# A perceiver layer with routed experts: the first expert's first block of rows is put together on chip by matrix products, and the expert counts are taken earlier

## The chip, the cores and the metric

The kernel runs on one core of one Trainium2 chip. Its time is the device time of one execution in microseconds (us). The core has five engines that run side by side, each with its own queue of instructions in a fixed order: TensorE (PE, with PEld for its weight loads) multiplies matrices, VectorE (DVE) and ScalarE (ACT) work on elements, GpSimd (POOL) does some element work and issues transfers, SyncE (SP) issues transfers. In the profile a name with a q at its end (PEldq, ACTq) stands for the engine's sequencer: register loads, waits and branches.

## The reference, cut to what matters

There are 8 x 64 = 512 tokens of 512 features. Three stages are added one after the other onto the tokens x:

```
x = x + cross_attention(layernorm(x), context)   # 8 contexts of 1601 rows
x = x + self_attention(layernorm(x))             # within each group of 64 tokens, 8 heads
x = x + experts(layernorm(x))

# experts, for each token:
logits = xn @ router_w.T + router_b              # 8 experts
val, idx = top_k(logits, 2);  weight = softmax(val)
out = sum over the two experts e of weight * (silu(h1) * h2) @ w2[e].T + b2[e]
      where h1, h2 = split(xn @ w1[e].T + b1[e])  # 2 x 2048 hidden
```

The reference runs all experts on all tokens and picks two. The kernel runs each expert only on the tokens that chose it. All arithmetic is in float32.

## The kernel before, in words

**Tiles.** The 512 tokens are NTT = 4 tiles of P = 128 tokens, tile t in `xs[t]`. Features are ND = 4 blocks of 128.

**Attention and routing.** For each tile there are generators: `scores` and `average` (cross attention), `mix`, `attend` and `route`. `run` interleaves them: each yields an estimate of how long it should be left alone, and `run` keeps a clock of the estimated product time. All products and transposes of this stage go through `matmul` (line 205) and `transpose` (line 201), which chain each one behind the one before it, so TensorE's order is the order in which they are written down. The order on the other engines is the compiler's scheduler's. Tiles 0 and 1 follow each other inside `others`, beside the cross attention of later tiles; tile 2 and then tile 3 come at the end. Tile 3's buffers lie in a pool of their own (`beside`), opened when the cross attention is over.

**route(t).** A layernorm gives `xn` (named `xr`), four transposes and four small products give the logits. VectorE ranks the 8 experts of each token and writes a 0/1 mask of the two chosen (`masks`, L548). Then `pos` counts, by products with a triangle (`tri`) and with ones over earlier tiles, how many earlier tokens chose the same expert. `told[:, 0]` (L570) is that place plus `e * 512`, `told[:, 1]` the softmax weight. From these come `place` (L580) and `weight` (L581), and two indirect transfers (L583, on POOL) scatter the rows of `xn` into `sorted_x` in device memory, where the rows of expert e start at row `e * 512`. Last, `tg` turns the weights around, ScalarE copies them to `gT`, the product `mm` with `b2` is added to `xs[t]` (L603).

**Counts.** After all stages, four products with a column of ones (`cnt`, L704) sum the masks, and VectorE writes them as integers to `counts` (L705). Each of PE, ACT, DVE and POOL loads all eight into registers, one at a time (L888).

**Experts.** Each expert has 12 weight panels of 1 MB, 8 of w1 and 4 of w2, read by SP (`load_panel`, L153) into two pools: `early` holds 9 of each 17 panels, and its first filling is issued right after the cross attention, `late` holds 8. For expert e and block j of 128 of its rows, `level(e, j, xT)` branches on the count: with at most 64 rows in the block `narrow` is run, else `dense`, and after `dense` perhaps `level(e, j + 1)`. `load_rows_of` (L725, on POOL) reads 128 rows of `sorted_x`, behind all scatters; `turn` (L740, L751) transposes them. Rows of block 0 are read up to two experts ahead and turned one ahead; those of block j + 1 are read while block j is computed. For expert 0 the rows are read and turned inside the chosen arm (`xn0` or `xd0`). `dense` makes 16 products groups `h` (L769), each closed by a Silu on ScalarE (L777) and a product on VectorE (L780), with two `h` buffers, then 16 wide products `o` (L791), copied by ScalarE (L795) and written to `sorted_y`. `narrow` does the same for 64 rows (L812, L843).

**End.** Both result rows of each token are gathered from `sorted_y`, multiplied with their weights and added to `xs[t]`.

Of the kernel before, what the change touches and what calls it, by code (L numbers as in the profile page):

```python
# [9 lines left out]
F32 = mybir.dt.float32  # L10
AF = mybir.ActivationFunctionType
ALU = mybir.AluOpType
# [3 lines left out]
P = 128  # L16
# [4 lines left out]
def tile_perceiver_layer(  # L21
# [27 lines left out]
    nc = tc.nc  # L49
    B, T, D = x.shape  # L50
    S = context.shape[1]
    NT = B * T
    NTT = NT // P
    ND = D // P
    H = 8
    HD = D // H
    E = b2.shape[0]
# [9 lines left out]
    const = ctx.enter_context(tc.tile_pool(name="const", bufs=1))  # L67
    small = ctx.enter_context(tc.tile_pool(name="small", bufs=2))


    ident = const.tile([P, P], F32, name="ident")
# [4 lines left out]
    xs = [const.tile([P, D], F32, name=f"xs{t}") for t in range(NTT)]  # L76
# [21 lines left out]
    b2_sb = const.tile([E, D], F32, name="b2_sb")  # L98
# [15 lines left out]
    for e in range(1, E):  # L114
# [8 lines left out]
        channel_multiplier=-1,  # L123
    )
    ones = const.tile([P, P], F32, name="ones")
    nc.gpsimd.memset(ones, 1.0)

    first = const.tile([P, E], F32, name="first")
    for e in range(E):
        nc.gpsimd.memset(first[:, e : e + 1], float(e * NT))  # L130
    masks = const.tile([P, NTT, E], F32, name="masks")
    place = const.tile([P, NTT, 2], mybir.dt.int32, name="place")
    weight = const.tile([P, NTT, 2], F32, name="weight")
    counts = const.tile([1, E], mybir.dt.int32, name="counts")
    scatters = []

# [34 lines left out]
    with ExitStack() as attn:  # L173
        wide_const = attn.enter_context(tc.tile_pool(name="wide_const", bufs=1))
        wpool = attn.enter_context(tc.tile_pool(name="wpool", bufs=5))
        tok = attn.enter_context(tc.tile_pool(name="tok", bufs=2))
        wide = attn.enter_context(tc.tile_pool(name="wide", bufs=1))
        ps = attn.enter_context(tc.tile_pool(name="ps", bufs=1, space=PSUM))
# [25 lines left out]
        def matmul(out, lhsT, rhs, **flags):  # L204
            in_line(nc.tensor.matmul(out, lhsT, rhs, **flags))  # L205
            columns = math.prod(out.shape[1:])
            clock[0] += max(0.12, columns * (1.8e-3 if out.shape[0] > T else 1.0e-3))
# [8 lines left out]
        def bank(t, shape, use, name):  # L216
            if t < NTT - 1 or not cross_done:
                tag, bufs = {"turn": ("tr", 1), "few": ("s", 1)}.get(use, ("mm", 2))
            else:
                tag, bufs = {"turn": ("ctr", 2), "few": ("csc", 1), "left": ("ctr", 2)}.get(use, ("av", 1))  # L220
            return ps.tile(shape, F32, tag=tag, name=name, bufs=bufs)

        def buffers(t):
            return wide if t < NTT - 1 or not cross_done else beside[0]
# [155 lines left out]
        def average(t):  # L380

            nmax = small.tile([P, 1], F32, tag="nmax", name="nmax")
            nc.vector.tensor_reduce(nmax, mxs[t], AX.X, ALU.max, negate=True)
            ssum = small.tile([P, 1], F32, tag="ssum", name="ssum")
            nc.scalar.activation(scs[t], scs[t], AF.Exp, bias=nmax, accum_out=ssum)
            rsum = small.tile([P, 1], F32, tag="rsum", name="rsum")
            nc.vector.reciprocal(rsum, ssum)
            yield 5.0
            av = ps.tile([P, D], F32, tag="av", name="av")
            pTs = {}  # L390
            for j in range(NSB + 1):
                if j < NSB:
                    n = min(SB, S - j * SB)
                    w = min(P, n)
                    nch = -(-n // P)
                    tr = ps.tile([P, SB // P, P], F32, tag="ctr", name="ptr", bufs=2)
                    for c in range(nch):
                        s0 = j * SB + c * P
                        transpose(tr[:w, c, :], scs[t][:, s0 : s0 + w], ident)
                    pT = tpool.tile([P, SB // P, P], F32, tag="pT", name="pT")  # L400
                    nc.vector.tensor_copy(pT[:w, :nch, :], tr[:w, :nch, :])
                    pTs[j] = pT, w, nch
                    yield 1.0 if j == 0 else 0.0
                if j > 0:
                    pT, w, nch = pTs[j - 1]
                    for c in range(nch):
                        for i in range(2):
                            matmul(
                                av[i * T : (i + 1) * T, :],
                                pT[:w, c, i * T : (i + 1) * T],  # L410
                                cs[t, j - 1, i][:w, c, :],
                                start=(j == 1 and c == 0),
                                stop=(j == NSB and c == nch - 1),
                            )
                        yield 0.0
            avgs[t] = tok.tile([P, D], F32, tag="avg", name="avg")
            nc.vector.tensor_scalar(avgs[t], av, rsum, None, ALU.mult)

        avgs = {}
# [102 lines left out]

        masked = []


        def route(t):
            xn = buffers(t).tile([P, D], F32, tag="xr", name="xr", bufs=pair(t))
            layernorm(xn, xs[t])
# [21 lines left out]
            yield 2.0  # L550
            while len(masked) < t:
                yield 0.5
            pos = bank(t, [P, E], "few", "pos")
            for u in range(t + 1):
                matmul(
# [12 lines left out]
            nc.vector.reciprocal(norm, norm)  # L568
            nc.vector.tensor_scalar(told[:, 1, :], told[:, 1, :], norm, None, ALU.mult)
            nc.vector.tensor_tensor(told[:, 0, :], pos, first, ALU.add)  # L570
            both = small.tile([P, 2, 2, E], F32, tag="both", name="both", bufs=2)
            nc.vector.tensor_tensor(
                both,
# [8 lines left out]
            for c in range(2):  # L582
# [7 lines left out]
                for other in scatters:  # L590
                    tc.declare_no_dep(scatter.ins, other.ins, reason="no two tokens share a row")
                scatters.append(scatter)
            yield 2.0


            tg = bank(t, [E, P], "turn", "tg")
# [102 lines left out]
        weights = []  # L699
        run(others(), cross_steps, rest_of([2]), rest_of([3]))  # L700

        cnt = ps.tile([1, E], F32, tag="s", name="cnt")
        for t in range(NTT):
            matmul(cnt, ones[:, 0:1], masks[:, t, :], start=(t == 0), stop=(t == NTT - 1))  # L704
        nc.vector.tensor_copy(counts, cnt)  # L705

    with ExitStack() as ffn:
# [12 lines left out]
        def load_rows_of(e, j):  # L722
            r = rows.tile([P, D], F32, tag="r", name="r")
            at = e * NT + j * P
            read = nc.gpsimd.dma_start(out=r, in_=sorted_x[at : at + P, :])  # L725
            for scatter in scatters:
                tc.add_manual_dep(
                    read.ins,
                    scatter.ins.name,
                    mybir.DependencyInfo(  # L730
                        mybir.DependencyClass.Sync, mybir.DependencyReason.DATA
                    ),
                    reason="rows of any tile",
                )
            return r

        def turn(r, tag, after=None):
            tr = banks.tile([P, ND, P], F32, tag="t" + tag[0] + tag[-1], name="t")
            for k in range(ND):
                turning = nc.tensor.transpose(tr[:, k, :], r[:, k * P : (k + 1) * P], ident)  # L740
                if after is not None:
                    tc.add_manual_dep(
                        turning.ins,
                        after.ins.name,
                        mybir.DependencyInfo(
                            mybir.DependencyClass.NoSync, mybir.DependencyReason.DATA
                        ),
                        reason="TensorE's program",
                    )
            xT = cols.tile([P, ND, P], F32, tag=tag, name=tag, bufs={"xT": NB - 1, "x0": 2}.get(tag, 1))  # L750
            nc.vector.tensor_copy(xT, tr)  # L751
            return xT

# [112 lines left out]
        def level(e, j, xT):  # L866
            n = held[e]
            with arm(n <= j * P + P // 2, f"narrow_{e}_{j}"):  # L868
                foretell(n > j * P + P // 2, f"dense_{e}_{j}")
                narrow(e, j, xT or turn(firsts[0], "xn0"))  # L870
            if j == 0:
                tc.no_sync_barrier()
            with arm(n > j * P + P // 2, f"dense_{e}_{j}"):  # L873
                if j + 1 < NB:
                    foretell(n > (j + 1) * P, f"more_{e}_{j}")
                ahead = dense(e, j, xT or turn(firsts[0], "xd0"))
                if j + 1 < NB:
                    with arm(n > (j + 1) * P, f"more_{e}_{j}"):
                        level(e, j + 1, ahead)
            if j == 0:  # L880
                tc.no_sync_barrier()

        def ask(n):
            while len(panels) < min(E * NPAN, n):
                load_panel(len(panels))

        held = [
            nc.values_load(counts[0:1, e : e + 1], engines=engines, min_val=0, max_val=NT)  # L888
            for e in range(E)
        ]  # L890
        ask(EARLY + LATE)
        firsts = [load_rows_of(e, 0) for e in range(3)]

        tc.no_sync_barrier()
        level(0, 0, None)
        turned_rows = [None]
        for e in range(1, E):
            ask(e * NPAN + EARLY + LATE)
            if e + 2 < E:
# [86 lines left out]
```

## Time and profile before

| | |
|---|---|
| median of 3 runs (lowest to highest) | 905.05 us (903.5 to 906.7) |
| the profiled execution, its time | 905.28 us |
| its span, first to last instruction | 903.5 us |
| mean granted TensorE clock | 0.932 |
| TensorE matmul busy | 771.2 us (85%) |
| VectorE / ScalarE / GpSimd busy | 225.9 / 159.6 / 66.9 us |
| bytes moved | 165.99 MB, mean 184 GB/s |

A timeline row gives the start, the busy time, the engine, the line and operation, the output and inputs by the program's names, the shapes, the count, and in brackets the idle time of the engine before it and what ended it. A row of one line's instructions gives the shortest, median and longest duration in ns, then the first and last start in us. Every time in a row is counted from the span's start. The profile is one execution, so sums are made against its own 905.28 us.

In that execution expert 0 runs `dense` for one block, experts 1 and 2 `narrow`, 3 and 4 `dense`, 5 `narrow`, 6 three `dense` blocks and a `narrow` one, 7 a `dense` and a `narrow` one.

### The profile page before, as it was taken

To read this page: it belongs to the slowest core of one execution; us is meant where nothing else is said; L and a number is where in the kernel's file an instruction comes from. 1 tells how busy PE (TensorE), PEld (TensorE's weight loads), DVE (VectorE), ACT (ScalarE), POOL (GpSimd) and SP (SyncE) were. 2 spreads that over 40 slices of the span, in tenths; PEclk is the share of its full clock that TensorE was granted. 3 is DMA by queue.
4 is the path that set the end of the run, shared out by engine and by line. 5 is a ranking of instruction groups with operands and counts; after the bars stand their busy time and mean duration, and the time that the engine had idled before them with its cause. 6 is when DMAs were issued, how large, how long until landed. Compare 5 with 4: busy or idle time off the path is not lost. (4 is left out here: it accounts for less than half of the span.)

```text
span 903.5 us, 11522 instructions
## 1 busy us (share of the span) xinstructions
PE 771.2 (85%) x4794; PEld 517.8 (57%) x4794; DVE 225.9 (25%) x514; ACT 159.6 (18%) x324; POOL 66.9 (7%) x114
## 2 busy tenths in 40 slices
PE   3997997997999874399998896998899999969980
PEld 3883544444454442297454875945878786559450
DVE  2322265255342464111111110201111111101012
ACT  1123144034132123021110111100111110012000
POOL 5100200300000000100000000000000000000003
PEclk9998998999899997589999898999899999979995
DMA  9930970790420821900899957749940000062004
GB/s 304 363 135 1 366 298 0 266 415 7 151 71 1 332 88 57 396 15 2 324 403 417 403 206 302 294 155 419 408 181 24 3 24 1 1 266 93 12 5 142
DMA packets 40315, 165.99 MB, mean 184 GB/s; under 512 B 3552, under 2 KB 3568, under 8 KB 27936
## 3 DMA queue, kind: packets, MB, share of 16 engines
q1 hardware_dynamic: 31968, 136.34, 38.9%
q0 software_dynamic: 8256, 28.42, 8.3%
q8 instruction: 59, 0.97, 0.4%
q14 instruction: 32, 0.26, 0.1%
HBM read 142.34 MB, written 22.41 MB: 182 GB/s over the span
## 5 line engine op out<-in xcount | busy, mean ns | idle before, releaser
L769 PE MATMUL h<-x,panel 128*128 128x128 f32 x1024 | 124.6, 288 | 22.1 <-PEq L868 21.4
L769 PEld LDWEIGHTS h<-x,panel 128*128 128x128 f32 x1024 | 123.4, 204 | 23.9 <-issue 22.6
L780 DVE SCALAR_TENSOR_TENSOR g<-h,b_sb,g 128x128 f32<-128x128 f32 x112 | 39.3, 351 | 232.3 <-ACT g L777 232.3
L791 PE MATMUL o<-panel,g 128*128 128x512 f32 x224 | 97.3, 592 | 0.0
L791 PEld LDWEIGHTS o<-panel,g 128*128 128x128 f32 x224 | 42.1, 190 | 50.2 <-issue 50.2
L777 ACT ACTIVATE g<-h,b_sb 128x128 f32<-128x128 f32 x112 | 41.1, 367 | 150.3 <-PE h L769 150.2
L201 PEld LDWEIGHTS ctr<-ident,c 128*128 128x128 f32 x384 | 43.1, 145 | 40.6 <-DVE cT L333 13.3
L201 PE MATMUL ctr<-ident,c 128*128 128x128 f32 x384 | 54.4, 286 | 13.1 <-DMA c<-in_context_dram 11.5
L769 PEld LDWEIGHTS h<-xT,panel 128*128 128x128 f32 x512 | 57.3, 192 | 2.8 <-issue 2.8
L769 PE MATMUL h<-xT,panel 128*128 128x128 f32 x512 | 57.6, 276 | 1.2 <-ACTq L868 0.6
L205 PE MATMUL sc_ps<-cT,qk 128*64 128x512 f32 (+1 forms) x256 | 54.4, 524 | 4.9 <-ACT sc L326 4.9
L333 DVE COPY cT<-ctr 128x512 f32<-128x512 f32 (+1 forms) x52 | 34.8, 670 | 61.6 <-PE ctr L201 61.2
L812 PE MATMUL hn<-panel,x 128*64 128x512 f32 x192 | 49.3, 605 | 0.0
L331 ACT COPY cT<-ctr 128x512 f32<-128x512 f32 (+1 forms) x52 | 29.6, 570 | 111.2 <-PE ctr L201 111.2
L205 PE MATMUL av<-c,pT 128*64 128x512 f32 x192 | 48.4, 642 | 0.0
L843 PE MATMUL on<-panel,gT 128*64 128x256 f32 x320 | 38.6, 381 | 0.0
L833 DVE TENSOR_TENSOR gn<-hn,gn 128x256 f32<-128x256 f32 x20 | 8.5, 425 | 103.3 <-ACT gn L832 97.7
L205 PEld LDWEIGHTS mm<-hT,w 128*128 128x128 f32 x256 | 29.2, 192 | 8.8 <-DVE hT L237 8.8
L205 PE MATMUL mm<-hT,w 128*128 128x128 f32 x256 | 30.7, 278 | 4.0 <-DVE hT L237 4.0
L812 PE MATMUL hn<-panel,xT 128*64 128x512 f32 x128 | 32.2, 596 | 0.0
L769 PE MATMUL h<-xd,panel 128*128 128x128 f32 x256 | 31.3, 288 | 0.8 <-DVE xd L751 0.8
L843 PEld LDWEIGHTS on<-panel,gT 128*64 128x64 f32 x320 | 24.5, 137 | 12.9 <-issue 0.8
(175 smaller groups left out, 703.2 us busy)
## 6 DMA issues: line engine op xcount, KB each, us to landing
panel<-in_w_dram SPq DMA_DIRECT2D x96, 1024.0 KB, 15.6
c<-in_context_dram SPq DMA_DIRECT2D x24, 1024.0 KB, 10.9
sorted_x<-zeros POOLq DMA_DIRECT2D x8, 1024.0 KB, 19.1
sorted_y<-zeros POOLq DMA_DIRECT2D x8, 1024.0 KB, 18.9
r<-sorted_x POOLq DMA_DIRECT2D x15, 256.0 KB, 6.6
sorted_y<-y POOLq DMA_DIRECT2D x7, 256.0 KB, 6.8
cl<-in_context_dram SPq DMA_DIRECT2D x8, 130.0 KB
xs<-in_x_dram SPq DMA_DIRECT2D x4, 256.0 KB, 8.4
```

The costliest lines, as they stand in the source:

```text
L201: in_line(nc.tensor.transpose(out, in_, identity))
L205: in_line(nc.tensor.matmul(out, lhsT, rhs, **flags))
L331: nc.scalar.copy(dst, tr)
L333: nc.vector.tensor_copy(dst, tr)
L769: last = nc.tensor.matmul(h[:, half, :], w[:, k, half, (n % PC) * P : (n % PC + 1) * P], xT[:, k, :], start=(k == 0), stop=(k == ND - 1),)
L777: nc.scalar.activation(g[:, n, :], h[:, 0, :], AF.Silu, bias=b1_sb[:, col : col + 1])
L780: nc.vector.scalar_tensor_tensor(g[:, n, :], h[:, 1, :], b1_sb[:, col + NC1 : col + NC1 + 1], g[:, n, :], ALU.add, ALU.mult,)
L791: nc.tensor.matmul(o, g[:, n, :], w2_chunk(e, n), start=(n == 0), stop=(n == NC1 - 1))
L812: nc.tensor.matmul(h[q * s : (q + 1) * s].rearrange("p h c d -> p (h c d)"), xT[:, k, :s], w[:, k, :], start=(k == 0), stop=(k == ND - 1),)
L833: nc.vector.tensor_tensor(gn, h[:, 1], gn, ALU.mult)
L843: nc.tensor.matmul(o[q * s : (q + 1) * s, :], gT[:, m, c, i * s : (i + 1) * s], w2_chunk(e, n)[:, q * W : (q + 1) * W], start=(n == 0), st ...
```

## The change

Four things are done differently.

- In `route`, each tile builds `taken`, a 128 x 128 matrix of zeros and ones: row p has its one in the column of the place that token p has among expert 0's rows, if it chose expert 0 and the place is below 128. Four products of the blocks of `xn` with `taken` give those rows already transposed. They are summed over the tiles in `xT0`, which takes the place of the rows read back and turned for expert 0's block 0. The scatters stay.
- For the last tile, the counts are taken as soon as the masks are there, ahead of `pos`.
- Before expert 0, each engine loads the count of expert 0 alone. The other seven are loaded in one instruction behind expert 0, without the run-time check of their bounds.
- The last tile's `tg`, `gT` and `mm`, with the addition to its `xs`, move from `route` to behind expert 0. There `mm` uses the bank of the transposes of expert 1's and 2's rows (`tx0`).

In the built program TensorE has the last tile's work in the order cnt, pos, put, the load of one count, the branch. VectorE has the addition into `xT0` ahead of `place` and `weight` in tile 3, and between `told` and the softmax of tile 3 in tile 2. Behind expert 0 ScalarE has a table load and then the copy to `gT`; TensorE has tg, mm, eight transposes and the load of seven counts.

```diff
+    slots = const.tile([P, P], F32, name="slots")
+    nc.gpsimd.iota(
+        slots, pattern=[[1, P]], base=0, channel_multiplier=0, allow_small_or_imprecise_dtypes=True
+    )
+    xT0 = const.tile([P, ND, P], F32, name="xT0")
...
-            avgs[t] = tok.tile([P, D], F32, tag="avg", name="avg")
+            avgs[t] = tok.tile([P, D], F32, tag="avg", name="avg", bufs=1)
...
+            if t == NTT - 1:
+                while len(masked) < NTT:
+                    yield 0.5
+                cnt = bank(t, [1, E], "turn", "cnt")
+                for u in range(NTT):
+                    matmul(cnt, ones[:, 0:1], masks[:, u, :], start=(u == 0), stop=(u == NTT - 1))
+                nc.vector.tensor_copy(counts, cnt)
             pos = bank(t, [P, E], "few", "pos")
...
             nc.vector.tensor_tensor(told[:, 0, :], pos, first, ALU.add)
+            taken = buffers(t).tile([P, H, HD], F32, tag="lk", name="taken", bufs=2)
+            taken = taken.rearrange("p h d -> p (h d)")[:, :P]
+            nc.vector.tensor_scalar(
+                taken, slots, told[:, 0, 0:1], masks[:, t, 0:1], ALU.is_equal, ALU.mult
+            )
...
-            yield 2.0
+            yield 1.0
+            put = bank(t, [P, ND, P], "", "put")
+            for k in range(ND):
+                matmul(put[:, k, :], xn[:, k * P : (k + 1) * P], taken, start=True, stop=True)
+            if t == 0:
+                nc.vector.tensor_copy(xT0, put)
+            else:
+                nc.vector.tensor_tensor(xT0, put, xT0, ALU.add)
+            if t == NTT - 1:
+                gates.append(told)
+                return
+            yield 1.0
...
-        cnt = ps.tile([1, E], F32, tag="s", name="cnt")
-        for t in range(NTT):
-            matmul(cnt, ones[:, 0:1], masks[:, t, :], start=(t == 0), stop=(t == NTT - 1))
-        nc.vector.tensor_copy(counts, cnt)
...
-                narrow(e, j, xT or turn(firsts[0], "xn0"))
+                narrow(e, j, xT)
...
-                ahead = dense(e, j, xT or turn(firsts[0], "xd0"))
+                ahead = dense(e, j, xT)
...
-        held = [
-            nc.values_load(counts[0:1, e : e + 1], engines=engines, min_val=0, max_val=NT)
-            for e in range(E)
-        ]
+        def load_counts(first, end):
+            _, values = nc.values_load_multi_w_load_instructions(
+                counts[0:1, first:end],
+                engines=engines,
+                min_val=0,
+                max_val=NT,
+                skip_runtime_bounds_check_because="an expert has at most all tokens",
+            )
+            return list(values)
+
+        held = load_counts(0, 1)
         ask(EARLY + LATE)
-        firsts = [load_rows_of(e, 0) for e in range(3)]
-
+        firsts = [None] + [load_rows_of(e, 0) for e in (1, 2)]
         tc.no_sync_barrier()
-        level(0, 0, None)
-        turned_rows = [None]
+        level(0, 0, xT0)
+        held += load_counts(1, E)
+
+        tg = banks.tile([E, P], F32, tag="o", name="tg")
+        nc.tensor.transpose(tg, gates[0][:, 1, :], ident)
+        gT = small.tile([E, P], F32, tag="gT", name="gT", bufs=2)
+        nc.scalar.copy(gT, tg)
+        mm = banks.tile([P, D], F32, tag="tx0", name="mm")
+        nc.tensor.matmul(mm, gT, b2_sb, start=True, stop=True)
+        nc.vector.tensor_tensor(xs[NTT - 1], mm, xs[NTT - 1], ALU.add)
+        turned_rows = [xT0]
```

More of the change, by code (lines that the diff above doesn't have):

```diff
@@ L135, in tile_perceiver_layer @@
     scatters = []
+    gates = []
     dram = ctx.enter_context(tc.tile_pool(name="dram", bufs=1, space=bass.MemoryType.DRAM))
@@ L749, in turn @@
                     )
-            xT = cols.tile([P, ND, P], F32, tag=tag, name=tag, bufs={"xT": NB - 1, "x0": 2}.get(tag, 1))
+            xT = cols.tile([P, ND, P], F32, tag=tag, name=tag, bufs=NB - 1 if tag == "xT" else 2)
             nc.vector.tensor_copy(xT, tr)
```

## The prediction

> **What bounds the kernel now.** I read the page first: TensorE is busy in 85% of the span, so only work on its path counts. The chain of waits covers just the end (gather, add, store, 2% of the span), which the change leaves alone. So I read the timeline from the last tile's routing to the first expert's products.
>
> ```profile
> 365.99 0.17 DVE L548 TENSOR_SCALAR masks<-rank 128x8 f32<-128x8 f32 x1
> 366.21 0.59 PE L205 MATMUL pos<-masks,tri 128*128 128x8 f32 x2
> 369.94 0.97 POOL L583 DMA_INDIRECT sorted_x<-xr,place  x1 [0.30 <-issue]
> 371.24 0.14 DVE L705 CAST counts<-cnt 1x8 int32<-1x8 f32 x1
> 378.95 1.69 POOL L725 DMA_DIRECT2D r<-sorted_x  x3 [8.03 <-DMA sorted_x<-xr,place]
> 384.84 1.09 PE L740 MATMUL t<-ident,r 128*128 128x128 f32 x4 [13.96 <-DMA r<-sorted_x]
> 386.76 13.44 PE L769 MATMUL h<-xd,panel 128*128 128x128 f32 x96 [0.84 <-DVE xd L751]
> 390.69 1.28 ACT L777 ACT_TABLE_LOAD   x1 [22.22 <-PE h L769]
> 392.39 0.35 DVE L780 SCALAR_TENSOR_TENSOR g<-h,b_sb,g 128x128 f32<-128x128 f32 x1 [5.68 <-ACT g L777]
> ```
>
> See: the last scatter lands 8.03 us after its issue ends (378.94), then the rows are read back, and TensorE idles 13.96 us. The first product starts at 386.76, the first gate product at 392.39. The instructions of L868 (the test whether expert 0 is narrow) show a second wait beside it:
>
> ```profile
> L868 PEldq COMPARE_BRANCH  x1: 6102/6102/6102, 377.6 to 377.6; - x1
> L868 PEldq EVENT_SEMAPHORE  x1: 51/51/51, 383.8 to 383.8; - x1
> ```
>
> The branch goes to the dense arm and takes 6.1 us, to 383.7. It is hidden behind the read-back, but only just. From 435 us on the experts follow each other with TensorE 9.7 to 10 of 10 us busy, idle at taken branches alone: no expert waits for its panels. What the first expert gains passes to the end, and what is put between experts is lost in full.
>
> **1. The first expert's start: gain 9 us.** At the last tile, cnt now stands before pos and holds the three ones products, which before ran ahead of the mask (1.45 us at 364.84, six passes), behind it. From the mask at 366.16: these 1.45 and tri's 0.59 end at about 368.3, told at 368.5 (0.17). taken is a 128x128 TENSOR_SCALAR; the rows are 0.23 us for 128x8 (L569) and 0.55 for 128x512 (L158), so 0.3: 368.8. put is four products, eight passes; transposes x8 at half clock took 1.97 us (L201 pr_ps), so 1.9: 370.7. Adding to xT0 takes 0.69 (L603): rows ready at 371.45. tg, its copy, mm and xs no longer stand here.
>
> TensorE's queue behind put: one load of a count instead of eight (they took 371.4 to 377.6; one takes 0.30 to 0.55), then the branch. Sequencing runs ahead of the array, so the branch starts near 369.6. Five other long branches of this test and the next (L868, L873) took 3.2, 3.5, 5.7, 5.8 and 6.9 us. The Trainium skill (Runtime: NRT & Kernel Launch, "Instruction fetch mechanics") says that a taken branch to code outside the fetched blocks stalls for a DMA fetch. The trace agrees that it costs, with a 16 KB packet in the instruction queue at 381 to 382. By the rule the stall comes back in full, uncovered: 369.6 + 6.1 + 0.75 to the first product (as after other branches) = 376.4; by the shortest row, 3.2, or a block already there, 372.5. Either way the start is 10 to 14 us earlier.
>
> But that is not what decides. ScalarE's first Silu table load waits, besides the first product, for both scatters of the last tile (its buffer lies where their source lay). VectorE now does the xT0 add ahead of place and weight, which therefore end at 371.75 instead of 368.47, and the scatters are issued 3.3 us later, to about 374.2. Landing took 8.03 us behind the full panel queue (the DMA share is 1.0 until 382); the median over the four scatters of tiles 2 and 3 was 5.1. I take 8, the row nearest to it: 382.2 at most, say 381.5. Then table load 1.28 and Silu 0.37: first gate product at 383.2 instead of 392.39. With two h buffers TensorE has two blocks done 5.7 us after its start and waits for that. Gain **9.2**; between 12 (landing in 5) and 7 (see the clock, below).
>
> The read of row block 0 goes from POOL; two reads, one count and its branch remain there, and the reads start 3.3 us later. They are for experts 1 and 2, 60 us on: hidden. The other block's rows are needed 30 us later: hidden. SP's order is the same.
>
> **2. put at the earlier tiles: loss 4.9 us.** Each of tiles 0 to 2 adds taken, four products and a copy or add.
>
> ```profile
> 158.58 0.16 DVE L570 TENSOR_TENSOR told<-pos,first 128x8 f32<-128x8 f32 x1
> 158.81 0.24 PEld L205 LDWEIGHTS av<-c,pT 128*64 128x64 f32 x2 [0.62 <-issue]
> ...
> 341.10 0.17 DVE L570 TENSOR_TENSOR told<-pos,first 128x8 f32<-128x8 f32 x1 [0.54 <-PE pos L205]
> ...
> 342.31 0.20 DVE L490 RECIPROCAL sumh<-sumh 128x8 f32<-128x8 f32 x1
> ...
> 344.61 0.37 PE L201 MATMUL tg<-ident,told 128*8 128x128 f32 x1 [3.55 <-DVE told L569]
> ```
>
> Tiles 0 and 1 route while TensorE is full with the next tile's average (PE 10.0 of 10 us in 160:170, 9.3 to 10 in most later stretches). put stands behind two av products, ready for it at about 158.8, and taken ends at 159.2: a stall of 0.3 to 0.4 and eight passes of 0.11 to 0.2. 1.4 and 1.5 us; no slack follows, so all of it passes on. At tile 2 VectorE's order is told, taken, sumh, told, xT0 add, reciprocal. The add must wait for put, and tile 3's softmax is queued behind it: taken to 341.6, put (half clock, 1.9) to 343.5, add to 344.25, so the reciprocal starts then instead of at 342.31: 2.0 us on the serial chain of tile 3. Sum 4.9; 3.5 if a third is absorbed, 6 with a cold clock.
>
> **3. What is put between expert 0 and 1: loss 5 us.**
>
> ```profile
> 432.28 0.58 ACT L795 COPY y<-o 128x512 f32<-128x512 f32 x1 [13.80 <-PE o L791]
> 433.32 0.63 PE L740 MATMUL t<-ident,r 128*128 128x128 f32 x4 [1.07 <-PEq L878]
> 434.04 0.69 DVE L751 COPY x<-t 128x512 f32<-128x512 f32 x1 [14.58 <-PE t L740]
> 435.37 1.57 PE L812 MATMUL hn<-panel,x 128*64 128x512 f32 x4
> ```
>
> Before, two transposes and copies and then expert 1 at 435.37. Now tg comes first (0.3); ScalarE, which ended y at 432.86, loads a table (1.28) and copies gT (0.25) to 434.65; mm (1.12 at full clock) to 435.8; VectorE adds it to xs (0.69) to 436.55, and as mm and t share a bank the first transpose waits for that. Then transpose, copy and second transpose as before (about 1.85 with a colder clock) to 438.4. Behind its wait stands the load of seven counts, ahead of expert 1's branch. A single load took 0.30 at least, so seven would be 2.1 and the sum 5.7; the same section of the skill gives about 200 ns a register even in bulk, by which an estimate is 1.4 and the sum 5.0. I take 1.4, as it is one instruction; bounds 0.4 and 2.2. Expert 1 starts at 440.4: **5.0** later (4 to 6). Removing the eight loads at the front is counted in part 1.
>
> **Clock.** By windows of 2 us the granted clock is 0.50 from 362 to 390. The skill (TensorE: Matmul & The Clock Gate, "HAM oscillation") says that an idle gap over some 3.4 us halves the clock. This speaks against the change: if the products start at 372.5, TensorE has two blocks done by 378.2, idles until 383.5 for ScalarE and starts cold a second time; the row to price it is the cold start at 386.76, 4.6 us at half clock, 2.3 us lost. If they start at 376.4 the idle time is 1.5 us and nothing is lost. I count none and keep 2.3 for a rival. iota, slots, the smaller average buffer and the one-tile routing order elsewhere cost nothing: iota runs under the first loads, and each average is transposed before the next is written (274.48 against 296.9).
>
> **Sum.** 9.2 - 4.9 - 5.0 = 0.7 us slower than the profiled run's own 905.28 (span 903.5): 906.0. The median of the runs shown is 905.05, 0.23 lower, which is 905.8. I say **906**. About 0.3%, 2.7 us, is what a measurement here can tell from no change.
>
> **Rivals.** (a) Likeliest, 42%: as above, 906, own range 903.5 to 907.7: no measurable change. (b) Slower, 29%: the second cold start. Place: between the second and third h block of expert 0. Price 2.3 us, so 908.3; it decides once TensorE is idle there for more than about 3.4 us, that is when the branch costs under 5 us. For it: two of six long branches cost 3.2 and 3.5; against it: the one at this very place cost 6.1. (c) Faster, 18%: the puts are absorbed. If tiles 0 to 2 cost nothing, 906 - 4.9 = 901.1; with a scatter landing in 5 us, 3 more, 898. For it: TensorE has idle slots of 0.5 to 2.3 us before tile 1's and 3's transposes; against it: each of them is released by VectorE or ScalarE work that itself follows a product. (d) Slower, 9%: the code before the experts grew, so later branches meet other block borders. Two branches that cost 3.2 and 3.5 becoming 6.5 gives 6.3 us, 912; it can also go the other way. That the rows don't come from put at all, or that the panels bound the first expert, is excluded: its w1 panels lie in the pool filled from 296.9 us on.
>
> **How the numbers follow.** Faster 0.18 (c), slower 0.40 (b, d and 2% of both signs), same 0.42. Range: 901 (c without the early landing) to 911 (b with 6 and 6 for parts 2 and 3), leaving out the ends of (c) and (d).
>
> **What would show it.** Right: h<-xT0 starts 10 to 14 us earlier relative to the mask, the branch of L868's successor is uncovered, ScalarE's first table load ends an idle time released by the scatter, not by h; tile 3's reciprocal stands 2 us later; tg, mm and seven counts take 5 us before expert 1. Wrong: the table load follows the first product at once, so that the gain is 12 or more; or the average stage's end doesn't move.

## The result, and the profile after the change

The changed kernel takes 911.13 us (median of six runs), the kernel before 905.82. One of the six took 1208.93 us, with a granted clock of 0.64 instead of 0.92 to 0.93; the five others took 909.6 to 912.9 us (median 910.89), and with these five the changed kernel takes 1.0062 times as long, 95% interval 1.0036 to 1.0089. A second set of 16 runs gave a median of 910.79 against 904.12, ratio 1.0065 (1.0042 to 1.0087). So it is slower by 5 to 7 us; 906.0 was forecast, 0.7 us slower. The ratios, here and below, are not exactly the quotients of the medians beside them.

The timeline of the changed kernel around the last tile's mask and the first expert (start, length, engine, line, operation; in brackets the idle time before it and what ended it). `put`, `taken` and `xT` are the change's own; a "first gate product" is the first g of VectorE (L808), and a transfer "lands" when its data have arrived:

```profile
373.76 0.17 DVE L555 TENSOR_SCALAR masks<-rank 128x8 f32<-128x8 f32 x1
374.11 1.45 PE L213 MATMUL pos<-masks,ones 128*128 128x8 f32 x6
374.22 0.15 DVE L566 CAST counts<-cnt 1x8 int32<-1x8 f32 x1
376.63 2.07 PE L213 MATMUL put<-taken,xr 128*128 128x128 f32 x8 [0.64 <-DVE taken L589]
378.74 0.69 DVE L621 TENSOR_TENSOR xT<-put,xT 128x512 f32<-128x512 f32 x1 [0.98 <-PE put L213]
379.34 0.16 DVE L601 CAST place<-found 128x2 int32<-128x2 f32 x1
379.53 6.76 PE L797 MATMUL h<-xT,panel 128*128 128x128 f32 x32 [0.83 <-DVE place L601]
381.06 0.97 POOL L604 DMA_INDIRECT sorted_x<-xr,place  x1 [0.30 <-issue]
390.82 1.28 ACT L805 ACT_TABLE_LOAD   x1 [17.47 <-DMA sorted_x<-xr,place]
391.64 1.16 POOL L753 DMA_DIRECT2D r<-sorted_x  x2 [9.61 <-DMA sorted_x<-xr,place]
392.52 0.61 DVE L808 SCALAR_TENSOR_TENSOR g<-h,b_sb,g 128x128 f32<-128x128 f32 x2 [12.95 <-ACT g L805]
392.93 3.26 PE L797 MATMUL h<-xT,panel 128*128 128x128 f32 x14 [6.63 <-DVE g L808]
```

The mask stands 7.77 us later than before. The first h product follows it by 5.77 us instead of 20.77. Then ScalarE's table load waits until the scatters have landed, 8.79 us after the second one's issue ended (382.03), and TensorE, with two h blocks done, idles for 6.63 us. The first gate product comes 18.76 us after the mask instead of 26.40. Behind that idle time TensorE starts cold, that is at half clock, a second time (a window: length; busy time and count of PE, PEld, DVE, ACT and POOL; granted clock; share of the DMA engines; GB/s):

```profile
393.53:395.53 2.00, 2.00 (x11) 2.00 (x11) 0.00 (x0) 0.00 (x0) 0.54 (x1) 0.50 0.54 211
```

The instructions of the test for expert 0 (L896) on TensorE's queue; nanoseconds, then the start:

```profile
L896 PEldq COMPARE_BRANCH  x1: 459/459/459, 377.2 to 377.2; - x1
L896 PEldq EVENT_SEMAPHORE  x1: 51/51/51, 378.7 to 378.7; - x1
```

The branch that took 6.1 us before takes 0.46. It starts while put still runs, as the prediction had it, and is done before xT0 is. At tile 2 the same timeline shows VectorE waiting for put in front of tile 3's softmax, 3.39 us from told to the reciprocal instead of 1.21:

```profile
346.52 0.17 DVE L584 TENSOR_TENSOR told<-pos,first 128x8 f32<-128x8 f32 x1 [0.54 <-PE pos L213]
346.73 0.35 DVE L589 TENSOR_SCALAR taken<-slots,told,masks 128x128 f32<-128x128 f32 x1
347.22 2.05 PE L213 MATMUL put<-taken,xr 128*128 128x128 f32 x8 [0.73 <-DVE taken L589]
349.30 0.69 DVE L621 TENSOR_TENSOR xT<-put,xT 128x512 f32<-128x512 f32 x1 [1.53 <-PE put L213]
349.91 0.19 DVE L498 RECIPROCAL sumh<-sumh 128x8 f32<-128x8 f32 x1
```

Between expert 0 and expert 1 the timeline reads as follows; below it stands the row of the two count loads on TensorE's queue, one count and then seven (shortest/median/longest in ns, first and last start):

```profile
433.85 0.59 ACT L823 COPY y<-o 128x512 f32<-128x512 f32 x1 [13.80 <-PE o L819]
434.53 0.27 PE L933 MATMUL tg<-ident,told 128*8 128x128 f32 x1 [0.72 <-ACTq L906]
434.69 1.28 ACT L935 ACT_TABLE_LOAD   x1 [0.26 <-ACTq L906]
436.29 1.48 PE L937 MATMUL mm<-b_sb,gT 8*128 8x512 f32 x2 [1.49 <-ACT gT L935]
437.81 0.69 DVE L938 TENSOR_TENSOR xs<-mm,xs 128x512 f32<-128x512 f32 x1 [16.79 <-PE mm L937]
438.56 1.11 PE L768 MATMUL t<-ident,r 128*128 128x128 f32 x4 [0.79 <-DVE xs L938]
440.45 1.12 PE L768 MATMUL t<-ident,r 128*128 128x128 f32 x4 [0.78 <-DVE x L779]
442.84 1.97 PE L840 MATMUL hn<-panel,x 128*64 128x512 f32 x4 [1.27 <-issue]
```

```profile
L916 PEldq TENSOR_LOAD <-counts x2: 495/1121/1747, 376.6 to 440.5; - x2
```

Expert 1 starts 8.99 us after y instead of 3.09. The transposes run at half clock (1.11 and 1.12 us instead of 0.63 and 0.66), and the seven counts take 1.75 us on TensorE's queue, from 440.5 on, beside the second transpose.

The spans by stretches, the second profile of the changed kernel being one of the experiments:

| stretch (us) | before | after | again |
|---|---|---|---|
| start to the last mask | 365.99 | 373.76 | 372.60 |
| mask to first gate product | 26.40 | 18.76 | 17.91 |
| first gate product to first o product | 25.96 | 27.39 | 27.79 |
| first o product to expert 1 | 17.02 | 22.93 | 22.47 |
| expert 1 to the end | 468.13 | 466.36 | 467.33 |
| span | 903.5 | 909.2 | 908.1 |

For the first pair: 7.77 - 7.64 + 1.43 + 5.91 - 1.77 = 5.70.

### The profile page after: what moved, and what is told of

The parts are those of the page before. It is cut to its first block, busy times and chain, and to the rows that moved or that the text cites. A ratio compares the mean times of both kernels' runs of the same rounds, so it can differ in the third digit from the quotient of the medians.

```text
span 909.2 us, 11533 instructions
## 1 busy us (share of the span) xinstructions
PE 781.3 (86%) x4822; PEld 526.1 (58%) x4822; DVE 229.0 (25%) x521; ACT 161.0 (18%) x325; POOL 66.6 (7%) x114
## 5 line engine op out<-in xcount | busy, mean ns | idle before, releaser
L808 DVE SCALAR_TENSOR_TENSOR g<-h,b_sb,g 128x128 f32<-128x128 f32 x112 | 39.2, 351 | 243.6 <-ACT g L805 243.5
L797 PE MATMUL h<-xT,panel 128*128 128x128 f32 x768 | 91.1, 283 | 8.7 <-DVE g L808 6.6
L797 PEld LDWEIGHTS h<-xT,panel 128*128 128x128 f32 x768 | 90.4, 200 | 10.8 <-DVE g L808 6.8
L213 PE MATMUL mm<-w,hT 128*128 128x512 f32 x64 | 28.5, 599 | 2.8 <-DVE hT L245 2.8
```

What stands on the lines that cost most here:

```text
L797: last = nc.tensor.matmul(h[:, half, :], w[:, k, half, (n % PC) * P : (n % PC + 1) * P], xT[:, k, :], start=(k == 0), stop=(k == ND - 1),)
L808: nc.vector.scalar_tensor_tensor(g[:, n, :], h[:, 1, :], b1_sb[:, col + NC1 : col + NC1 + 1], g[:, n, :], ALU.add, ALU.mult,)
```

## The experiments

All ratios are against the kernel before, run on the same chip in the same set, with 95% intervals. The changed kernel's own ratio, to compare them with, is 1.0065.

**Rows apart.** My theory: the wait for the scatters holds the first expert. The rival: something else would hold it next.

```diff
-            xn = buffers(t).tile([P, D], F32, tag="xr", ...)
+            rows_of = buffers(t) if buffers(t) is wide else last_rows[0]   # a pool that is never given up
+            xn = rows_of.tile([P, D], F32, tag="xr", ...)
```

> The changed kernel, with the last tile's normalized rows in a place of their own, so that what the experts' pools reuse is no longer read by the two scatters. Nothing is left out. Theory (the scatters' landing holds ScalarE's first table load, and through it the first gate product): the table load follows the first h block, the first gate product comes about 5.7 us after the first h product as it did before the change, about 19.4 us after the mask's start minus 8: near 385.3 instead of 392.5, and with no idle time over 1 us TensorE does not fall back to half clock a second time. 7.2 and 1.4 us: 902.5 us, faster than before the change by about 3. Rival (another thing holds the table load, or what is won is lost again in a later wait for the second row block or the panels): within 2 us of the changed kernel's 911.

901.03 us, ratio 0.9970 (0.9949 to 0.9991). Its timeline:

```profile
375.37 5.43 PE L799 MATMUL h<-xT,panel 128*128 128x128 f32 x32 [0.83 <-DVE place L602]
379.16 1.28 ACT L807 ACT_TABLE_LOAD   x1 [9.96 <-PE h L799]
381.26 25.28 PE L799 MATMUL h<-xT,panel 128*128 128x128 f32 x224 [0.46 <-DVE g L810]
```

The table load is released by the first h block. The first gate product (380.86) comes 11.26 us after the mask (369.60), TensorE idles 0.46 us, and the h products from there to the next transposes take 25.12 us instead of 26.54 to 26.95. The theory holds: 8.5 to 8.9 us of the changed kernel's stretch from mask to o (45.7 and 46.2 us, here 37.2) were this wait and the cold start behind it. What makes the wait is the pool. In both built programs g lies at the same bytes of each partition (134432 to 142624) and so does xr (153568 to 155616); they do not overlap, and all that differs is the pool that xr belongs to. In the changed kernel it is `beside`, in whose place g lies and which is given up as a whole. The prediction, with "its buffer lies where their source lay", put this too narrowly.

**Bias last, and counts at once.** These two price what stands between expert 0 and 1.

```diff
             level(e, 0, turned_rows[e])
+        tg ... gT ... mm ... xs[NTT - 1] += mm        # moved from before the loop over experts 1 to 7
```

> The changed kernel, with the last tile's bias product (tg, its copy gT, mm and the add to xs) not between expert 0 and 1 but behind the last expert, where TensorE has nothing to do while the last rows come back. Nothing is left out. Theory (this product stands on the path in full): expert 1's first product comes 3.5 to 4.5 us earlier after the end of expert 0; 907 us. The load of seven counts stays where it was and keeps its 1.7 us. Rival (the seven counts are what the gap consists of, and the product lies beside them): under 1 us, 910 to 911.

906.41 us, ratio 1.0015 (0.9996 to 1.0035). From the first o product to expert 1 it is 18.62 us: 3.9 to 4.3 less, within the 3.5 to 4.5 expected.

```diff
-        held = load_counts(0, 1)
+        held = load_counts(0, E)
...
-        held += load_counts(1, E)
```

> The changed kernel, with all eight counts loaded by one instruction ahead of expert 0 instead of one there and seven behind expert 0. Nothing is left out. Theory (the seven cost 1.75 us on TensorE's queue between the experts; eight at once cost about 1.95 ahead of expert 0, where TensorE's sequencer waits for put and the xT0 add): 1.3 to 1.8 us faster, 909.4. Rival (eight delay the branch and so the first product by 1.4 us, no gain): 911.

905.96 us, ratio 1.0017 (0.9998 to 1.0036): some 4 us less, where 1.3 to 1.8 were expected. Between the experts it is 21.45 us, 1.0 to 1.5 less, a little under what was expected. The rest came from an order that I had not meant to change: VectorE now does place and weight ahead of the xT0 add.

```profile
374.32 0.16 DVE L602 COPY weight<-found 128x2 f32<-128x2 f32 x1
374.69 0.97 POOL L604 DMA_INDIRECT sorted_x<-xr,place  x1 [22.89 <-DVE weight L602]
375.40 0.69 DVE L621 TENSOR_TENSOR xT<-put,xT 128x512 f32<-128x512 f32 x1 [0.92 <-PE put L213]
```

The first scatter is issued 4.28 us after the mask (370.41) instead of 6.02, and the first gate product comes after 15.88 us instead of 17.9 to 18.8. That supports the chain that the prediction named: add, place, scatter, landing, gate product. The run changes two things at once, so it does not price the order alone.

**No early put.** Leaves out taken, put and the add of tiles 0 to 2.

> The changed kernel without taken, put and the xT0 add of tiles 0 to 2: expert 0's first block holds only the last tile's rows, so that this part of the computation is left out. It prices the put of the earlier tiles. Prediction's step: 4.9 us earlier at the last mask. Theory now (from the mask's place in the two traces, 373.76 and 365.99): 7.8 us earlier at the mask, and so 903 to 903.5. Rival (absorbed; the mask comes later for another reason, such as the smaller average buffer): less than 3 us, 908 or more.

902.67 us, ratio 0.9963 (0.9942 to 0.9983). The mask stands at 364.63, 9.1 us earlier than in the first profile of the changed kernel. But one pair of profiles does not price this. From the end of tile 0's average to tile 2's mask the eight profiles that have the early puts took 245.1 to 249.0 us (mean 247.1), the five that lack them (this one, the kernel before, and three below) 241.7 to 245.7 (mean 243.7): 3.4 for tiles 0 and 1, but each set spreads by as much, so that by my estimate from these thirteen the 3.4 is uncertain by 2.3 either way. The spread goes with the granted clock over this stretch: it is 0.94 to 0.95 in the longer profiles of both sets and 0.96 in the shorter ones. Compared within the longer ones the difference is 3.2, within the shorter ones 3.0. From tile 2's mask to tile 3's the changed program takes 28.07 to 28.21 us, this one 25.84 and the kernel before 25.75: 2.3 for tile 2. Together 5.7, or 5.3 to 5.5 at like clock; the other 2 or so us of the first pair's 7.77 lie within that spread.

This run held a second answer. Its test for expert 0 takes 6.36 us, and TensorE waits for it (the test's line, then the timeline, then the window behind the idle time):

```profile
L894 PEldq COMPARE_BRANCH  x1: 6355/6355/6355, 368.1 to 368.1; - x1
```

```profile
375.21 6.05 PE L795 MATMUL h<-xT,panel 128*128 128x128 f32 x32 [5.64 <-PEq L894]
380.85 1.28 ACT L803 ACT_TABLE_LOAD   x1 [16.62 <-DMA sorted_x<-xr,place]
382.95 2.27 PE L795 MATMUL h<-xT,panel 128*128 128x128 f32 x18 [1.69 <-DVE g L806]
```

```profile
383.21:385.21 2.00, 2.00 (x20) 2.00 (x20) 0.00 (x0) 0.17 (x1) 0.54 (x1) 1.00 0.69 231
```

The h products start 10.58 us after the mask instead of 5.77, and yet the first gate product does not come later (17.92 us): the landing decides, as the prediction said. TensorE idles only 1.69 us, keeps its full clock, and loses nothing to a second cold start.

**The changed kernel again.**

> The changed kernel itself once more, beside the others of this set. In the profile taken first the last tile's mask stood 276.4 us behind the end of tile 0's average, while the three kernels with the same program up to that point (rows apart, bias last, counts at once) show 273.4 to 273.8, the one without early puts 267.5 and the kernel before 267.8. Theory now: 2.7 us of that first profile were a chance fall of the granted clock, and the early puts cost 5.9: expected here 273.5 between the two points and 910 to 911 us. Rival (the 7.8 us are this kernel's own): 276.

910.79 us, ratio 1.0065 (1.0042 to 1.0087). From tile 0's average to the last mask it is 277.04 us, so the rival's number came. Yet the kernel with three edits below, whose instructions are the same up to there, shows 277.1, and those of the first set 273.4 to 273.8. So it is neither the chance of one profile nor this kernel's own: the same instructions fall into one of two groups, some 3 us apart, and what chooses between them stays open. It is not the chip: the kernel of the next run, on the chip of this one and with the same instructions up to tile 2's mask, needs 245.5 us to that mask, this one 249.0.

**Tile 2's add late.**

```diff
-                nc.vector.tensor_tensor(xT0, put, xT0, ALU.add)
+                add = nc.vector.tensor_tensor(xT0, put, xT0, ALU.add)
+                if t == NTT - 2:
+                    tc.add_manual_dep(add.ins, <tile 3's last probs product>, NoSync, ...)
```

> The changed kernel with tile 2's xT0 add put on VectorE behind tile 3's softmax (reciprocal and the weighting of the probabilities) instead of ahead of it. Nothing is left out. Theory of the prediction (VectorE waits for put in front of tile 3's serial chain): from tile 2's mask to tile 3's mask 26.2 us, the 25.8 of before plus taken, instead of 28.2; some 2 us less, 908.5 to 909. Rival (TensorE's put products themselves stand in front of tile 3's products): 28.0 stays.

911.54 us, ratio 1.0074 (1.0048 to 1.0099): nothing gained. From mask to mask it is 28.97 us, longer than either theory had. The stall itself is gone, tile 3's reciprocal standing 2.08 us behind tile 2's mask instead of 4.24. But the last projection of tile 3 differs: first here, then in the changed kernel (windows over just this product, columns as above):

```profile
358.21:364.37 6.16, 6.16 (x8) 2.37 (x8) 0.00 (x0) 1.25 (x1) 0.00 (x0) 0.60 0.00 0
```

```profile
359.37:363.07 3.70, 3.70 (x8) 1.43 (x8) 0.00 (x0) 1.24 (x1) 0.00 (x0) 1.00 0.00 0
```

It started 12.12 us behind the mask instead of 13.70, and then took 2.46 us longer at a clock of 0.60. What the stall cost, the clock took instead. This is one profile; the median, no better than the changed kernel's, agrees with it.

**Three edits together**: rows apart, bias last, counts at once.

> The changed kernel with three of the edits together: the last tile's rows apart, its bias product behind the last expert, all eight counts at once. Nothing is left out. Theory (the three costs are separate places on one path): from 911, 8.9 for the scatter wait and the second cold start, 4.3 for the bias product, 1.5 for the counts: 896.3. Rival (they cover each other, or TensorE's branch to the dense arm, up to 6 us, now stands uncovered): 900 or more.

895.06 us, ratio 0.9883 (0.9821 to 0.9945). The three costs add up: 896.3 was expected, from 8.9, 4.3 and 1.5. What the counts gave on their own beyond these 1.5 does not come on top, since it shortened the same wait for the scatters that the rows apart remove.

**Read back.** These three edits, and instead of the early puts:

```diff
+            if t == NTT - 2:                                   # behind tile 2's scatters
+                nc.sync.dma_start(out=r0, in_=sorted_x[0:P, :])
...
+                for k in range(ND):                            # tile 3, ahead of cnt
+                    matmul(put[:, k, :], r0[:, k * P : (k + 1) * P], ident, start=(k == 0), stop=False)
...
+                    matmul(put[:, k, :], xn[:, k * P : (k + 1) * P], taken, start=False, stop=(k == ND - 1))
```

> As the one with three edits, and tiles 0 to 2 have no taken, put and xT0 add: row block 0 of sorted_x, as it stands after the scatters of tiles 0 to 2 (cleared rows where a token of tile 3 will go), is read back while tile 3 is in its attention, turned by four products with ident while TensorE waits for tile 3's mask, and tile 3's put is summed onto it in the same bank. Nothing is left out. Theory (the early puts cost 5.9, and what takes their place lies in TensorE's idle time): 890.5. Rival (the read-back lands after tile 3's mask and holds the counts' product behind it, or a taken branch comes uncovered): 895 or more.

891.06 us, ratio 0.9854 (0.9793 to 0.9914), near the 890.5 expected, but in part by luck. What its rival named is there too: the branch takes 6.1 us again and holds the first h product (the test's line, then the timeline). From mask to o this costs 4.6 us against the kernel with three edits (42.45 and 37.82), and what makes up for it was not in the expectation: expert 1 to the end takes 462.6 instead of 467.0 us.

```profile
L912 PEldq COMPARE_BRANCH  x1: 6108/6108/6108, 369.8 to 369.8; - x1
```

```profile
371.05 0.69 DVE L637 COPY xT<-put 128x512 f32<-128x512 f32 x1 [0.91 <-PE put L214]
376.61 31.28 PE L813 MATMUL h<-xT,panel 128*128 128x128 f32 x256 [5.60 <-PEq L912]
```

**Two kernels with code moved.** Products of 128x1 into a bank that nobody reads, at the start, only to move TensorE's later code:

```diff
+        for i in range(9):                                     # 55 in the second
+            in_line(nc.tensor.matmul(pad, ident, ident[:, 0:1], start=True, stop=True))
         opening = scores(0, 3)
```

> As the one with the read-back, with nine products of 128x1 into a bank that nobody reads at the very start, where TensorE waits for its first loads. They only move TensorE's later code by 35 instructions, so that the test for expert 0 stands where it stands in the changed kernel (0.46 us there, 6.1 us in the kernel with the read-back, in the one without early puts and in the kernel before). Nothing is left out. Theory (the place of the code in its fetched blocks decides whether the taken branch finds its target there): the branch takes under 1 us, the first h product follows the xT0 copy at 0.8 us instead of 4.9 us behind it: 886.2. Rival (the branch is long because it comes earlier after TensorE's busy stretch, or because of the panels' traffic): 6 us stay, 891.

889.52 us, ratio 0.9830 (0.9781 to 0.9879). The branch takes 0.46 us, and the first h product starts 0.80 us behind the start of the xT0 copy (376.23 and 377.03) instead of 5.56, so it is the branch's place in the code that makes it short, not its time. The 4.8 us gained there do not show in the time, since in the profiled run tile 3's last projection took 5.94 us instead of 3.70, and expert 2 to the end took 438.1 us instead of 432.9.

> The changed kernel with fifty-five such products at the start: its test for expert 0 is moved by 220 instructions[...]. Nothing is left out. Theory: the branch takes about 6 us again and the first h product comes 4 to 5 us later; but what decides is the landing of the scatters, so the first gate product stays where it was behind the mask (18.7 us), TensorE's idle time behind the second h block falls to about 2 us, it does not start cold a second time (the h products from there on take 25.3 instead of 26.7 to 27.1 us), and the time is the same or 1.4 us shorter: 909.5. Rival of the prediction (an uncovered branch is lost in full): 915.

922.88 us, ratio 1.0199 (1.0149 to 1.0249): neither. The fifty-five products were not hidden. Tile 0's average ends at 110.64 instead of 95.6 to 100.6, and from there to the end it is 811.9 us, as in the changed kernel's two profiles (811.8 and 812.5). The branch takes 6.44 us, the first h product stands 10.59 us behind the mask, and the first gate product 18.14, where it was: that half of the theory holds. The other half fell. TensorE idled only 1.87 us and still went cold (three windows around the idle time, columns as above, the clock being third from the end):

```profile
402.35:404.35 2.00, 2.00 (x15) 1.90 (x14) 0.00 (x0) 0.14 (x1) 0.00 (x0) 0.80 0.28 113
404.35:406.35 2.00, 0.13 (x2) 0.04 (x1) 0.45 (x2) 1.77 (x3) 1.16 (x2) 1.00 0.07 8
406.35:408.35 2.00, 2.00 (x10) 2.00 (x11) 0.17 (x1) 0.00 (x0) 0.54 (x1) 0.55 0.77 262
```

The run without early puts idled 1.69 us at this place and stayed at 1.00. A limit between the two would explain that, but the same trace speaks against it: at tile 3's attention TensorE idled longer, and the granted clock stayed at 1.00 over the idle time and the 10 us behind it, as it did at this place in all thirteen profiles (1.95 to 1.96 us).

```profile
333.35 3.70 PE L213 MATMUL mm<-w,vT 128*128 128x512 f32 x8 [1.95 <-ACT vT L271]
```

So the length of one idle time does not decide; what does stays open.

**The later tests moved back.** The kernel of nine products, and fifty-five products more in an arm that never runs, which move only the code behind expert 0.

> As the read-back kernel moved by 35 instructions, with fifty-five products more in an arm that this data never runs (the narrow arm of expert 0's second block), which moves TensorE's code behind expert 0 by 220 instructions. The test for expert 0 stays where its branch took under 1 us, and the later experts' tests stand again where they stood in the read-back kernel[...]. Nothing is left out. In the profile of the read-back kernel the stretch from expert 2's transpose to the end of the span took 432.9 us, in the moved one 438.1, with taken branches over 1 us adding up to 23.5 and 35.6 us there. Theory (these 5.2 us are the later branches, by their place in the blocks): 433 from expert 2 to the end, and 884.5 us. Rival (chance of one profile, or the clock): 438, and 889.5.

886.12 us (885.5 to 892.6), ratio 0.9810 (0.9783 to 0.9836), the fastest of all, and about 2.5% under the changed kernel. The time came near the 884.5 expected, but the reason did not show: in the profile, of an execution of 892.6 us, expert 2 to the end took 437.4 us, not 433, and the later branches were not short again. They stand some 255 instructions (35 and 220) further on than in the read-back kernel, which the expectation took for the same place. What makes those branches long stays open.

## Why the prediction was wrong

**The forecast of no measurable change failed on part 1, the first expert's start.** It was to gain 9.2 us and gained 6.2 (first profile) and 6.7 (second). Its chain was right in each link: the h products ahead of the scatters, the xT0 add ahead of place, the issue put back (it ended 8.27 us behind the mask, 8.2 forecast), the landing that holds ScalarE. The rows-apart run shows it by taking the link away. Two terms were mis-sized.

- The second cold start, at "I count none". The prediction took the branch at its full 6.1 us, which left TensorE 1.5 us of idle time behind the second h block. The branch took 0.46 us, the idle time was 6.63 and 5.79, and the cold start behind it cost 1.43 and 1.83 us between the first gate product and o. That is rival (b), at its place, below its price of 2.3. This is the step that failed.
- The landing. The row says 8, but the sum has 7.3 (374.2 to 381.5). It took 7.95 to 8.79 us in the five profiles with this order, 1.5 more than the sum has in the first and 0.7 in the second. (The 5.1 of the early landing is a median of two unlike pairs: tile 2's scatters took 2.73 us each from issue to landing, tile 3's 7.5 and 8.1.)

**Rival (b)'s point of decision** was an idle time over 3.4 us, the rule of the Trainium skill (TensorE: Matmul & The Clock Gate, "HAM oscillation"). In the changed kernel the idle time was 5.8 to 6.6, so here the rule held, but the moved kernel went cold after 1.87 us. The price of the branch, 6.1 in one case and 3.2 in the other, was outside what happened (0.46 us). The prediction allowed for it only by the words "or a block already there", and gave it too little weight. Two of its readings made that easier. By its own numbers the idle time passes 3.4 us once the branch costs under 4, not 5 (383.5 - 3.4 - 5.7 - 0.75 - 369.6 = 4.05). And where it names five other long branches, the trace has eight over 1 us on those two lines: 1.7, 3.2, 3.5, 3.7, 5.7, 5.8, 6.5 and 6.9. Short ones were less rare than it says.

**Part 2** (4.9): the mean over the profiles is 5.7, 3.4 for tiles 0 and 1 (2.9 forecast; 3.0 to 3.2 at like clock) and 2.3 for tile 2 (2.0 forecast). Its size was right within what these profiles can tell; the 7.77 us of the first pair overstate it. The mechanism named for tile 2 is in the trace, but taking it away gained nothing.

**Part 3** (5.0): 5.9 and 5.5. The terms that the prediction names end at 439.8, not 440.4, so 0.6 of its 5.0 has no name. Counted from the end of y, expert 1 came 0.86 us later in the first profile than forecast (8.40 and 7.54). Of these, 0.36 are mm, which took 1.48 us for 1.12, at a mean clock of 0.72. Another 0.35 are the seven counts: 1.75 us, not the 1.4 that the prediction worked out from the 200 ns a register of the Trainium skill (Runtime: NRT & Kernel Launch, "Instruction fetch mechanics"), but within its bounds. The two transposes and the copy between them took 3.01 us, where 1.85 was allowed "as before" (before they took 2.12); this hardly adds to the sum, because the load of the counts runs beside the second transpose and not behind it.

**Sum.** With means: -6.4 + 5.7 + 5.7 = 5.0, against 0.7 forecast; measured 5.1 and 6.7. So 2.8 of the 4.3 us missing are part 1, the others 0.8 and 0.7, of which the 0.8 of part 2 is within its uncertainty. **Rival (c)**, puts absorbed, is excluded by the run without them. **Rival (d)**, later branches at other places, made no loss between these two kernels (expert 1 to the end was 0.8 to 1.8 us shorter, which the sum leaves out), though between the three-edit and the read-back kernel that stretch differs by 4.4 us.

## What to carry to other kernels

When a product no longer needs a transfer, look for what else still waits for that transfer: here a pool given up as a whole kept a table load behind the scatters, and moving the scattered rows to a pool of their own gave 8.5 to 8.9 us in that stretch. Price each new gap on TensorE with a cold start behind it, also when it seems short (1.87 us was enough once here), and take durations of the work behind it at half clock. When a price depends on a branch, price both ends of what such branches took: here 0.46 and 6.1 us. Do not read a few us out of one pair of profiles: the same instructions here differed by 3.7 us in one stretch.

## What was not expected of the hardware

- The taken branch to expert 0's dense arm took 0.37 to 0.46 us in eight kernels and 6.1 to 6.4 us in four (the one before among them). Which it is went with the place of the code: some thirty-five instructions put in at the start made 6.11 into 0.46 us, and 220 made 0.46 into 6.44. Why the place matters, these runs do not show.
- Loading one count took 0.50 us on TensorE's queue, seven behind the first 1.75 us, and all eight in one instruction 0.79 us. It does not go by the number of registers.
- The granted clock fell after an idle time of 1.87 us in one run, held over 1.69 us at the same place in another, and held over 1.95 us elsewhere in the first. Removing a wait of 2 us ahead of a chain of products let them start 1.6 us earlier, and one of them ran 2.5 us longer at a clock of 0.60.
